# Second experts of a two-layer graph network: up to 12 units of up to 512 columns with arms chosen by token counts, rows turned by VectorE, and scatters that are not chained within an expert's unit

## The chip, the cores and the metric

The kernel runs on one core of a Trainium2 chip. A core has five engines with instruction streams of their own: TensorE (PE, with its weight loads as PEld), VectorE (DVE), ScalarE (ACT), GpSimd (POOL) and SyncE (SP). SP and ACT also issue plain DMAs, POOL also indirect ones (gathers and scatters by a list of row numbers). The metric is the device time of one execution in microseconds (us). The kernel before takes 3464.89 us, the median of three runs (3464.35 to 3468.28).

## The reference

Two layers work on 1250 rows (tokens, nodes of a graph) of 1024 float32. Each layer adds to x a graph convolution and an attention-like mix of the normalised x, then adds a mixture of experts of the normalised sum:

```python
xn = _layernorm(x)
x = x + gcn(xn, edges) + spherical_attention(xn)
x = x + experts0(_layernorm(x))          # 8 experts, capacity 391, width 512
xn = _layernorm(x)
x = x + sage(xn, edges) + linear_attention(xn)
x = x + experts1(_layernorm(x))          # the change is about this one
```

The second experts choose the two best of eight for each token and have no capacity, so that an expert can receive any number of tokens:

```python
scores = x @ gate_w.T                    # 1250 x 8
topk_scores, topk_idx = top_k(scores, 2)
p = softmax(topk_scores)
h1, h2 = split(x @ w12[e].T)             # w12[e]: 512 x 1024, two halves of 256
y += p * ((silu(h1) * h2) @ w3[e].T)     # w3[e]: 1024 x 256, for both chosen e
```

Worked out from the reference with its inputs, the eight experts of the second mixture receive 0, 276, 515, 394, 1, 557, 17 and 740 tokens, 2500 together. The first mixture's receive 318, 358, 263, 231, 330, 366, 397 and 237, of which 391 at most are kept.

## The kernel before

One function, `network`, holds the whole computation as one program. A scheduler orders the instructions of each engine; tiles from pools with a number of buffers set when a writer may start. [...] Weights of all stages share a pool of three buffers (`wpool`, tag "w"). A second call of `network` under `tc.If(many == 1)` is for inputs that do not occur here, and is not executed.

*First experts* (L780 to L899). Routing builds a table of token numbers with small matmuls (L753), and from it `idx`, `idx_q` and `taken`, the number of tokens of each expert. Expert 0's rows are gathered whole (L802), transposed by TensorE (L808) and copied by ACT and VectorE in turn (`evac`, L116 and L118). The rows of later experts are gathered as quarters of 1 KB (L816), laid out so that VectorE's 32x32 transposing (L825) gives the columns. `weights(e)` issues three loads of 2 MB on SP (gate, up, down; L844 is the down one), for expert 0 after the gathers of its rows in the program. Each engine reads `taken` into registers, and `by_width` chooses among four code arms (248, 296, 344, 392 columns) by comparing and branching: four times an expert for gate and up (L864 to L867), and twice for down (L884 to L886).

*Second routing* (L1072 to L1305). Two top scores of each token give one-hot rows; matmuls with a triangular matrix give each token's rank at its expert (`ahead`, from pR at L1158) and the experts' counts (pN). VectorE turns ranks into cells. A cell has 128 slots, and there are 27 of them (CELLS), a number that any distribution fits: ten pairs of cells with 256 slots each and seven single ones. The table of cells comes from float32 matmuls (L1292, `at` by `what`, over two choices and ten tiles of tokens) with three columns per cell: token, weight and expert. Cells that a small expert leaves partly empty are filled with tokens of weight zero: POOL computes `fill_at` (L1274), and matmuls (L1296) add it. From the table's PSUM come `unit_e` (the expert of each cell, L1298), `gate` and `idx`.

*Second experts* (L1309 to L1353). Ten pairs and seven singles form 17 units in a fixed order, each with 256 or 128 columns. A unit reads its expert's number on SP and loads w12 (2 MB, L1312) and w3 (1 MB); POOL gathers 128 rows of 4 KB per cell (L1320); TensorE transposes them (L1326), and evac copies them to `xeT`. Gate and up are 64 records of matmuls (L1333): two halves of hidden features, two banks, eight blocks of input features, each float32 matmul recorded twice. ACT applies silu, VectorE multiplies (L1337). Down is four matmuls (eight records) of 512 columns per cell (L1344); VectorE and ACT each scale half of it by the token's weight (L1349, L1347). POOL then scatters the rows with an add into the output in DRAM (L1350). All scatters write the same tensor, so each waits for the one before it to land.

Of the kernel before, what the change touches and what calls it, by code (L numbers as in the profile page):

```python
# [10 lines left out]
F32 = mybir.dt.float32  # L11
F32R = mybir.dt.float32r
# [10 lines left out]
P = 128  # L23
# [25 lines left out]
PAIRS = 10  # L49
CELLS = 27  # L50
UNITS = [u for i in range(PAIRS) for u in ((2 * i, 2), (2 * PAIRS + i, 1)) if u[0] < CELLS]
BLOCKS = 10
LN_EPS = 1e-5
# [49 lines left out]
def network(tc: tile.TileContext, a: dict, out: bass.AP, env: SimpleNamespace, exact: bool):  # L103
# [80 lines left out]
    def residual(pool, i, t, cols, bias):  # L184
# [4 lines left out]
        return xr  # L189

# [601 lines left out]
    with s_route:  # L792
        quarters = x1n_d.rearrange("n (j f) -> (n j) f", j=4)
        with tc.tile_pool(name="moe0", bufs=1) as mp:
# [34 lines left out]
            def by_width(n, widths, work):  # L829

                if len(widths) == 1:
                    return work(widths[0])
                m = len(widths) // 2
                with tc.If(n <= widths[m - 1]) as cmp:
                    by_width(n, widths[:m], work)
                with cmp.Else():
                    by_width(n, widths[m:], work)

            def weights(e):
# [4 lines left out]
                nc.sync.dma_start(wd, a["L0_ffn_down_w"][e].rearrange("(k p) f -> p k f", p=P))  # L844
# [57 lines left out]
    idx = mp1.tile([P, CELLS], I32, name="idx1")  # L902
    gate = mp1.tile([P, CELLS], F32, name="gate1")
    unit_e = mp1.tile([1, CELLS], I32, name="unit_e")
# [8 lines left out]
    expert = pk.tile([P, 2, T], F32, name="expert1")  # L913
# [171 lines left out]
    def choose1(t0, t1):  # L1085
# [3 lines left out]
        nc.vector.tensor_copy(expert[:, :, tt], ixf.rearrange("p t k -> p k t"))  # L1089
# [52 lines left out]


    with tc.tile_pool(name="cells", bufs=1) as cp:
# [6 lines left out]
        token = cp.tile([P, T], F32, name="token1")  # L1151
        nc.gpsimd.iota(token, pattern=[[P, T]], base=0, channel_multiplier=1, allow_small_or_imprecise_dtypes=True)
        count = cp.tile([P, P], F32, name="count1")
        nc.gpsimd.iota(count, pattern=[[1, P]], base=0, channel_multiplier=0, allow_small_or_imprecise_dtypes=True)
        pR = bank("pR")
# [13 lines left out]
        other = cp.tile([P, 2, E], F32, name="other")  # L1169
        nc.vector.tensor_scalar(other, both[:, 0:2, :], -1.0, 1.0, op0=OP.mult, op1=OP.add)  # L1170
# [3 lines left out]
        steps = cp.tile([P, BLOCKS], F32, name="steps")  # L1174
        nc.vector.tensor_scalar(steps, count[:, :BLOCKS], float(P), 0.5, op0=OP.mult, op1=OP.add)
        nc.vector.tensor_tensor(blocks, pN[:, :E].unsqueeze(2).to_broadcast([P, E, BLOCKS]),
                                steps.unsqueeze(1).to_broadcast([P, E, BLOCKS]), op=OP.is_gt)
        per = cp.tile([P, 3, E], F32, name="per")
        nb = cp.tile([P, E], F32, name="nb")
        nc.vector.tensor_reduce(nb, blocks, AX.X, OP.add)  # L1180
        evens = cp.tile([P, 5], F32, name="evens")
# [5 lines left out]
        for r in run:  # L1187
            nc.vector.memset(r, 0.0)
# [20 lines left out]
        def tmp(name):  # L1209
            return cp.tile([P, 2, T], F32, name=name)  # L1210
# [192 lines left out]
```

## Time and profile before

| | us |
|---|---|
| median of three runs | 3464.89 (3464.35 to 3468.28) |
| the profiled execution, own time | 3477.62 |
| its span in the trace | 3475.9 |
| TensorE busy | 3303.3 |
| VectorE, ACT, POOL busy | 915.1, 375.0, 591.1 |
| last matmul of the second graph layer ends | 3090.7 |
| first gate-and-up matmul of the second experts | 3144.17 |
| last matmul of the second experts ends | 3458.63 |
| last scatter issued | 3463.69 |

The granted TensorE clock is 0.97 of full speed in the mean. The profile is one execution, in microseconds from the start of its span. A group's row names the line, the engine, the operation, the tile written and the tiles read, shapes and count; after the bar come the busy time, the mean of one in ns, and the idle time of the engine just before the group with what ended it. Matmuls overlap in their records, so the length of a run of them is read from the timeline, where the start of one run and that of the next are seen. A line of the timeline has start, length, engine, line, operation and tiles, and in brackets the idle time before it.

### The profile page before, as it was taken

What the parts mean: (1) busy time and instruction counts of PE and PEld (TensorE: products, weight loads), DVE (VectorE), ACT (ScalarE), POOL (GpSimd) and SP (SyncE); (2) the same over time, 40 slices, a digit from 0 to 9 for tenths busy, and PEclk for the clock granted to TensorE, in tenths of its full rate; (3) what the DMA queues carried; (4) which work ended last, traced back from release to release, by engine and by line L of the source; (5) the groups of instructions that cost most, each with busy time, mean ns of one, the idle gap of its engine ahead of it and who ended that gap; (6) DMA issues with size and microseconds to landing.
All of it is one profiled execution on the core that took longest, in us unless ns stands there. A gap on an engine that the chain in (4) does not pass through costs nothing.

```text
span 3475.9 us, 31257 instructions
## 1 busy us (share of the span) xinstructions
PE 3303.3 (95%) x12399; PEld 2053.6 (59%) x12399; DVE 915.1 (26%) x2401; ACT 375.0 (11%) x662; POOL 591.1 (17%) x496
## 2 busy tenths in 40 slices
PE   6999999999998699999699999999999999988997
PEld 3474656654557456756355555457777454666775
DVE  4248335531114623231520000011111111341111
ACT  1001011100004111111110111000000000001111
POOL 0006786042001131210200000110000010022221
PEclk9999999999999599999899999999999999988999
DMA  4715222054104245554630000220100110319884
GB/s 153 170 56 130 25 1 26 25 190 139 53 25 166 76 141 196 156 184 116 212 107 25 25 25 25 93 104 1 49 1 25 64 45 18 109 57 304 277 262 102
DMA packets 165063, 343.51 MB, mean 99 GB/s; under 512 B 37467, under 2 KB 58882, under 8 KB 162684
## 3 DMA queue, kind: packets, MB, share of 16 engines
q1 hardware_dynamic: 101612, 247.26, 20.9%
q0 software_dynamic: 39616, 52.68, 7.4%
q10 hardware_dynamic: 23632, 40.77, 4.1%
q8 instruction: 138, 2.26, 0.3%
q14 instruction: 65, 0.53, 0.0%
HBM read 261.79 MB, written 78.87 MB: 98 GB/s over the span
## 4 chain that ended last, share of the span: by engine, by line
PE 52%; DMA 2%; DVE 1%; ACT 1%; issue 0%; POOL 0%; ACTq 0%; SPq 0%; POOLq 0%; DVEq 0%
PE ppn L164 8%; PE pqT L940 8%; PE p L1333 6%; PE pa L503 5%; PE ph L164 4%; PE pwo L164 4%; PE ph L1064 4%; PE py L1344 3%; PE pv L164 2%; PE py L884 2%; PE pgate L864 2%; PE pup L864 2%; DMA res_d<-xt 1%; DVE xt L971 1%; PE psc L1082 1%; PE pkv L999 1%
## 5 line engine op out<-in xcount | busy, mean ns | idle before, releaser
L265 POOL DMA_INDIRECT adj_d<-cnt,cell x167 | 259.9, 1556 | 90.7 <-issue 41.5
L1333 PE MATMUL p<-xeT,w 128*128 128x256 f32 (+1 forms) x1088 | 195.1, 340 | 5.4 <-ACT xeT L116 4.8
L1333 PEld LDWEIGHTS p<-xeT,w 128*128 128x128 f32 x1088 | 173.1, 192 | 26.3 <-ACT xeT L116 9.6
L188 POOL TENSOR_TENSOR xr<-xr,bo 128x512 f32<-128x512 f32 (+1 forms) x40 | 50.4, 1265 | 711.4 <-PE pwo L164 451.3
L864 PE MATMUL pgate<-xeT,wg 128*128 128x392 f32 (+3 forms) x512 | 154.3, 456 | 2.6 <-DVE py L886 2.0
L884 PE MATMUL py<-hT,wdb 128*128 128x392 f32 (+3 forms) x512 | 147.8, 448 | 8.2 <-DVE hT L867 4.1
L164 PE MATMUL pqk<-wk,x0T 128*128 128x512 f32 (+1 forms) x320 | 144.9, 607 | 9.5 <-ACT x0T L116 7.9
L864 PE MATMUL pup<-xeT,wu 128*128 128x392 f32 (+3 forms) x512 | 148.6, 442 | 2.2 <-issue 2.2
L164 PE MATMUL pv<-wv,x1T 128*128 128x512 f32 (+1 forms) x320 | 141.1, 598 | 7.5 <-ACT x1T L116 5.4
L164 PE MATMUL ph<-ws,h1T 128*128 128x512 f32 (+1 forms) x320 | 143.2, 596 | 0.0
L164 PE MATMUL pqk<-wq,x0T 128*128 128x512 f32 (+1 forms) x320 | 140.7, 593 | 0.0
L164 PE MATMUL ppn<-wn,x1T 128*128 128x256 f32 (+1 forms) x640 | 138.8, 379 | 0.0
L1064 PE MATMUL ph<-x1T,ws 128*128 128x416 f32 (+1 forms) x384 | 138.2, 512 | 0.0
L164 PE MATMUL pv<-wv,x0T 128*128 128x512 f32 (+1 forms) x320 | 138.0, 592 | 0.0
L164 PE MATMUL ph<-wgcn,x0T 128*128 128x512 f32 (+1 forms) x320 | 138.0, 593 | 0.0
L164 PE MATMUL pwo<-wo,attn0T 128*128 128x512 f32 (+1 forms) x320 | 137.7, 592 | 0.1
L164 PE MATMUL ppn<-wn,h1T 128*128 128x512 f32 (+1 forms) x320 | 137.7, 592 | 0.0
L164 PE MATMUL pwo<-wo,attn1T 128*128 128x512 f32 (+1 forms) x320 | 137.5, 592 | 0.0
L940 PE MATMUL pqT<-x1T,wk 128*128 128x416 f32 (+1 forms) x384 | 135.6, 512 | 0.0
L940 PE MATMUL pqT<-x1T,wq 128*128 128x416 f32 (+1 forms) x384 | 135.6, 512 | 0.0
L864 PEld LDWEIGHTS pgate<-xeT,wg 128*128 128x128 f32 x512 | 100.5, 197 | 52.6 <-issue 8.1
L884 PEld LDWEIGHTS py<-hT,wdb 128*128 128x128 f32 x512 | 97.6, 192 | 57.1 <-ACT wdb L874 6.6
(384 smaller groups left out, 4494.0 us busy)
## 6 DMA issues: line engine op xcount, KB each, us to landing
w<-in_L_ffn_w_dram SPq DMA_DIRECT2D x17, 2048.0 KB
w<-in_L_ffn_w_dram SPq DMA_DIRECT2D x17, 1024.0 KB
wg<-in_L_ffn_gate_w_dram SPq DMA_DIRECT2D x8, 2048.0 KB
wu<-in_L_ffn_up_w_dram SPq DMA_DIRECT2D x8, 2048.0 KB
wd<-in_L_ffn_down_w_dram SPq DMA_DIRECT2D x8, 2048.0 KB
y_d<-ye ACTq DMA_DIRECT2D x30, 416.0 KB
adj_d<-ezero SPq DMA_DIRECT2D x2, 6105.0 KB
res_d<-xr SPq DMA_DIRECT2D x45, 256.0 KB
```

Of the source, the lines that this page charges most:

```text
L164: nc.tensor.matmul(pr[:TS[t], :cols], xT[:, k, TOK[t]], w[:, k, :], start=(k == 0), stop=(k == nk - 1))
L188: nc.gpsimd.tensor_add(xr[:TS[t]], xr[:TS[t]], bias[:TS[t]])
L265: nc.gpsimd.indirect_dma_start(out=adj_d[e % 2], out_offset=bass.IndirectOffsetOnAxis(ap=cell[:, e:e + 1], axis=0), in_=cnt[:, e:e + 1], i ...
L503: nc.tensor.matmul(pa, edges if by_node else feats, feats if by_node else edges, start=(s == 0 and i == 0), stop=(s == T - 1 and i == len( ...
L864: nc.tensor.matmul(pw[:, :n], w[:, k, ic], xeT[:, k, :n], start=(k == 0), stop=(k == KB - 1))
L884: nc.tensor.matmul(py[:, :n], wdb[:, i, b, :], hT[:, i, :n], start=(i == 0), stop=(i == I0 // P - 1))
L940: nc.tensor.matmul(pq[:, :n], w[:, k, pair * P:(pair + 1) * P], xT[:, k, c0:c0 + n], start=(k == 0), stop=(k == KB - 1))
L971: nc.vector.scalar_tensor_tensor(xt[:ts], yt[:ts], env.wts[:ts, t, k:k + 1], xt[:ts], op0=OP.mult, op1=OP.add)
L999: nc.tensor.matmul(pkv[:, :P], kf[:TS[t], t, :], v[:TS[t], t, pair * P:(pair + 1) * P], start=(t == 0), stop=(t == T - 1))
L1064: nc.tensor.matmul(ps[:, :n], w[:, k, q0 + f * P:q0 + (f + 1) * P], xT[:, k, c0:c0 + n], start=(k == 0), stop=(k == KB - 1))
L1333: nc.tensor.matmul(pw_[:, :n], w12[:, k, off + i * P:off + (i + 1) * P], xeT[:, k, :n], start=(k == 0), stop=(k == KB - 1))
L1344: nc.tensor.matmul(py, hT[:, i, c * P:(c + 1) * P], w3[:, i, half * 512:(half + 1) * 512], start=(i == 0), stop=(i == H1 // P - 1))
```

## The change

The fixed grid of 27 cells gives way to at most 12 units (NU) of four blocks of 128 slots (UC). An expert with up to 512 tokens has one unit, one with more is shared evenly by blocks among two or three. Unit u's expert (`unit_e`) comes from the counts alone, ahead of the table. The table's matmuls are in float32r, with the weight cut into a high and a low part, in five steps behind VectorE's pieces; the filling of cells is gone. `taken` has the number of tokens of each unit, and `idx_q` the numbers of quarter rows as in the first experts.

In the units, `by_width` (moved to the top of `network`) chooses one of seven widths for gate and up in each half, and one of four numbers of blocks for gathering, turning and down. Only the first unit's rows are gathered whole and transposed by TensorE. For the others POOL gathers quarters up to two units ahead, and VectorE turns them. Units from the sixth on are skipped if empty. The first unit's weights are loaded by SP, the next two units' by ACT, the others' by SP; w12 is laid out with 16 KB in one piece for a partition. Empty slots of a table have a row number beyond the output, which the scatter leaves out, and scatters of one unit do not wait for each other.

In the first experts, the down weights of expert 0 are loaded by ACT's queue, and the load is kept in its place in the program's order. In ACT's stream as built it stands behind the four `evac` copies of expert 0's rows; POOL's stream as built has, before the units, the 12 quarter gathers of the second unit, the first block of the first unit, 8 quarter gathers of the third unit, and the other blocks of the first unit.

```diff
-PAIRS = 10
-CELLS = 27
-UNITS = [u for i in range(PAIRS) for u in ((2 * i, 2), (2 * PAIRS + i, 1)) if u[0] < CELLS]
 BLOCKS = 10
+UC = 4
+NU = 12
+COLS = NU * UC
+WIDTHS1 = [128, 192, 256, 320, 384, 448, 512]
+COUNTS = [P * (c + 1) for c in range(UC)]
...
+    def by_width(n, widths, work):
+        if len(widths) == 1:
+            return work(widths[0])
+        m = len(widths) // 2
+        with tc.If(n <= widths[m - 1]) as cmp:
+            by_width(n, widths[:m], work)
+        with cmp.Else():
+            by_width(n, widths[m:], work)
...
-                nc.sync.dma_start(wd, a["L0_ffn_down_w"][e].rearrange("(k p) f -> p k f", p=P))
+                load = (nc.sync if e else nc.scalar).dma_start(wd, a["L0_ffn_down_w"][e].rearrange("(k p) f -> p k f", p=P))
+                if e == 0:
+                    tc.keep_in_program_order(load)
...
-        fill = cp.tile([P, 2, E], F32, name="fill")
...
-        fill_at = cp.tile([P, 2, E, P], F32, name="fill_at")
-        for t in range(2):
-            for e in range(E):
-                nc.gpsimd.tensor_scalar(fill_at[:, t, e, :], count1, fill[:, t, e:e + 1], token1[:, t:t + 1],
-                                        op0=OP.is_equal, op1=OP.mult)
...
+        more = cp.tile([P, E], F32, name="more")
+        nc.vector.tensor_scalar(more, nb, UC + 0.5, None, op0=OP.is_gt)
+        units = run[0][:, 8:16]
+        nc.vector.scalar_tensor_tensor(units, nb, 0.5, more, op0=OP.is_gt, op1=OP.add)
+        nc.vector.scalar_tensor_tensor(units, nb, 2 * UC + 0.5, units, op0=OP.is_gt, op1=OP.add)
         for i, d in enumerate((1, 2, 4)):
+            nc.vector.tensor_add(run[1 - i % 2][:, 8:16], run[i % 2][:, 8:16], run[i % 2][:, 8 - d:16 - d])
+        of_unit = cp.tile([1, NU, E], F32, name="of_unit")
+        nc.vector.tensor_tensor(of_unit, count[0:1, :NU].unsqueeze(2).to_broadcast([1, NU, E]),
+                                run[1][0:1, 8:16].unsqueeze(1).to_broadcast([1, NU, E]), op=OP.is_ge)
+        its = cp.tile([1, NU], F32, name="its")
+        nc.vector.tensor_reduce(its, of_unit, AX.X, OP.add)
+        nc.vector.tensor_scalar(unit_e, its, E - 1.0, None, op0=OP.min)
...
-            for k in range(2):
-                nc.tensor.matmul(pt[:, :3 * CELLS], at[:TS[t], k, t, :], what[:TS[t], k, t].rearrange("p a g -> p (a g)"),
-                                 start=(t == 0 and k == 0), stop=False)
-        for t in range(2):
-            for e in range(E):
-                nc.tensor.matmul(pt[:, :CELLS], fill_at[:, t, e, :], fill_hit[:, e, :], start=False,
-                                 stop=(t == 1 and e == E - 1))
...
+        for t0 in range(0, T, 2):
+            tt = slice(t0, t0 + 2)
+            nc.vector.tensor_tensor(at[:, :, tt], count.unsqueeze(1).unsqueeze(1).to_broadcast([P, 2, 2, P]),
+                                    pos[:, :, tt].unsqueeze(3).to_broadcast([P, 2, 2, P]), op=OP.is_equal)
+            nc.vector.tensor_tensor(hit[:, :, tt], count[:, :COLS].unsqueeze(1).unsqueeze(1).to_broadcast([P, 2, 2, COLS]),
+                                    cell[:, :, tt].unsqueeze(3).to_broadcast([P, 2, 2, COLS]), op=OP.is_equal)
+            for j, v in enumerate((token1[:, tt].unsqueeze(1).unsqueeze(3).to_broadcast([P, 2, 2, COLS]),
+                                   w_hi[:, :, tt].bitcast(F32).unsqueeze(3).to_broadcast([P, 2, 2, COLS]),
+                                   w_lo[:, :, tt].unsqueeze(3).to_broadcast([P, 2, 2, COLS]))):
+                nc.vector.tensor_mul(what[:, :, tt, j, :], hit[:, :, tt], v)
+            for t in range(t0, t0 + 2):
+                for k in range(2):
+                    nc.tensor.matmul(pt[:, :3 * COLS], at[:TS[t], k, t, :],
+                                     what[:TS[t], k, t].rearrange("p a g -> p (a g)"),
+                                     start=(t == 0 and k == 0), stop=(t == T - 1 and k == 1))
...
+        used = cp.tile([P, COLS], F32R, name="used")
+        nc.vector.tensor_scalar(used, pt[:, :COLS], 0.5, None, op0=OP.is_gt)
+        pf = bank("pused")
+        nc.tensor.matmul(pf[:, :COLS], env.ones_r, used, start=True, stop=True)
+        took = cp.tile([1, NU], F32, name="took1")
+        nc.vector.tensor_reduce(took, pf[0:1, :COLS].rearrange("p (u c) -> p u c", c=UC), AX.X, OP.add)
+        nc.vector.tensor_copy(taken, took)
...
-        for c0, nc_ in UNITS:
-            n = nc_ * P
-            which = nc.values_load(unit_e[0:1, c0:c0 + 1], engines=(mybir.EngineType.SP,), min_val=0, max_val=E - 1)
-            w12 = wpool.tile([P, KB, 2 * H1], F32, name="w12", tag="w")
-            nc.sync.dma_start(w12, a["L1_ffn_w12"][bass.ds(which, 1)].rearrange("e (k p) f -> p (e k) f", p=P))
-            w3 = ep.tile([P, H1 // P, D], F32, name="w3")
-            nc.sync.dma_start(w3, a["L1_ffn_w3"][bass.ds(which, 1)].rearrange("e (k p) f -> p (e k) f", p=P))
-            xeT = ep.tile([P, KB, 2 * P], F32, name="xeT1")
-            for c in range(nc_):
-                xe = ep.tile([P, D], F32, name="xe1", bufs=4)
-                nc.gpsimd.indirect_dma_start(
-                    out=xe, out_offset=None, in_=env.x3n_d,
-                    in_offset=bass.IndirectOffsetOnAxis(ap=idx[:, c0 + c:c0 + c + 1], axis=0))
...
+        def load_unit(w, which, queue):
+            queue.dma_start(w[0], a["L1_ffn_w12"][bass.ds(which, 1)].rearrange("e (p k) f -> p (e k) f", k=KB))
+            queue.dma_start(w[1], a["L1_ffn_w3"][bass.ds(which, 1)].rearrange("e (k p) f -> p (e k) f", p=P))
...
+        ws = places()
+        load_unit(ws, expert_of(0, SP), nc.sync)
+        xe = ep.tile([P, UC, D], F32, name="xe1", bufs=1)
+        for c in range(UC):
+            nc.gpsimd.indirect_dma_start(
+                out=xe[:, c], out_offset=None, in_=env.x3n_d,
+                in_offset=bass.IndirectOffsetOnAxis(ap=idx[:, c:c + 1], axis=0))
+        number = [nc.values_load(taken[0:1, u:u + 1], min_val=0, max_val=UC * P) for u in range(NU)]
+        queues = [(nc.sync, SP) if u > 2 else (nc.scalar, ACT) for u in range(NU)]
+        which = [None] + [expert_of(u, queues[u][1]) for u in range(1, NU)]
+        def when(u, work):
+            if u < 5:
+                return work()
+            with tc.If(number[u] >= 1):
+                work()
+        xeT = ep.tile([P, KB, UC * P], F32, name="xeT1")
...
+        def fetch(u):
+            xq = ep.tile([P, UC * 4, B, KB], F32, name="xq1")
+            def work(n):
+                for i in range(n // B):
+                    nc.gpsimd.indirect_dma_start(
+                        out=xq[:, i].rearrange("p c b -> p (c b)"), out_offset=None, in_=quarters3,
+                        in_offset=bass.IndirectOffsetOnAxis(
+                            ap=idx_q[:, i % 4, u * UC + i // 4:u * UC + i // 4 + 1], axis=0))
+            when(u, lambda: by_width(number[u], COUNTS, work))
+            return xq
+        by_width(number[0], COUNTS, turn_first)
+        coming = [fetch(1)]
+        for u in range(NU):
+            later = u + 1 < NU
+            if u + 2 < NU:
+                coming.append(fetch(u + 2))
+            if later:
+                xq = coming.pop(0)
+                xeT2 = ep.tile([P, KB, UC * P], F32, name="xeT1")
+                ws2 = places()
+            w12, w3 = ws
+            hT = ep.tile([P, H1 // P, UC * P], F32, name="h3T")
+            def turn(n):
+                for c in range(n // P):
+                    i0, i1 = 4 * c, 4 * c + 4
+                    nc.vector.transpose(xeT2.rearrange("p b (i r) -> p i b r", r=B)[:, i0:i1],
+                                        xq[:, i0:i1].rearrange("p i c b -> p i b c"))
+            def unit():
+                if later:
+                    when(u + 1, lambda: load_unit(ws2, which[u + 1], queues[u + 1][0]))
+                for i in range(H1 // P):
+                    def gate_up(n):
+                        m = -(-n // P) * P
+                        p1, p2 = bank("p1"), bank("p2")
+                        for pw_, off in ((p1, 0), (p2, H1)):
+                            for k in range(KB):
+                                nc.tensor.matmul(pw_[:, :n], w12[:, k, off + i * P:off + (i + 1) * P], xeT[:, k, :n],
+                                                 start=(k == 0), stop=(k == KB - 1))
+                        sg = ep.tile([P, UC * P], F32, name="sg1")
+                        nc.scalar.activation(sg[:, :n], p1[:, :n], AF.Silu)
+                        nc.vector.tensor_mul(hT[:, i, :n], sg[:, :n], p2[:, :n])
+                        if n < m:
+                            nc.vector.memset(hT[:, i, n:m], 0.0)
+                    by_width(number[u], WIDTHS1, gate_up)
+                if later:
+                    when(u + 1, lambda: by_width(number[u + 1], COUNTS, turn))
+                def down(n):
+                    sent = []
+                    for c in range(n // P):
+                        ye = ep.tile([P, D], F32, name="ye1", bufs=6)
+                        own = gate[:, u * UC + c:u * UC + c + 1]
+                        for half in range(2):
+                            py = bank("py1")
+                            for i in range(H1 // P):
+                                nc.tensor.matmul(py, hT[:, i, c * P:(c + 1) * P], w3[:, i, half * 512:(half + 1) * 512],
+                                                 start=(i == 0), stop=(i == H1 // P - 1))
+                            if half:
+                                nc.scalar.activation(ye[:, 512:], py, AF.Copy, scale=own)
+                            else:
+                                nc.vector.tensor_scalar(ye[:, :512], py, own, None, op0=OP.mult)
+                        add = nc.gpsimd.indirect_dma_start(
+                            out=out, out_offset=bass.IndirectOffsetOnAxis(
+                                ap=idx_s[:, u * UC + c:u * UC + c + 1], axis=0),
+                            in_=ye, in_offset=None, bounds_check=N - 1, oob_is_err=False, compute_op=OP.add)
+                        for other in sent:
+                            tc.declare_no_dep(add.ins, other.ins, reason="no token is twice at an expert")
+                        sent.append(add)
+                by_width(number[u], COUNTS, down)
```

## The prediction

> **What bounds the kernel now.** I read the busy shares first, then the costliest groups, the chain that ended last, the stretches around the second experts, and last the order of instructions at their start and in the first experts.
>
> The page's first part and its row of TensorE's clock in 40 slices:
>
> ```profile
> PE 3303.3 (95%) x12399; PEld 2053.6 (59%) x12399; DVE 915.1 (26%) x2401; ACT 375.0 (11%) x662; POOL 591.1 (17%) x496
> PEclk9999999999999599999899999999999999988999
> ```
>
> TensorE is busy 95% of the span at nearly full clock, so in most places only fewer TensorE microseconds or a shorter gap count. Over the second experts (units from 3144 us to the end) the stretches say so too. Columns: busy time and count of PE, PEld, DVE, ACT, POOL, then clock, DMA share, GB/s.
>
> ```profile
> 3090.70:3144.20 53.50, 27.52 (x158) 25.96 (x156) 22.30 (x111) 5.17 (x10) 21.00 (x26) 0.54 0.28 102
> 3144.20:3435.70 291.50, 286.94 (x1410) 218.50 (x1411) 46.38 (x81) 39.51 (x80) 59.57 (x46) 0.99 0.83 259
> ```
>
> Routing (first row) keeps TensorE half idle. The units keep it 98% busy, with VectorE at 16%, POOL at 20%: there is room on these two to take TensorE's work. The units' groups by shape:
>
> ```profile
> L1333 PE MATMUL p<-xeT,w 128*128 128x256 f32 x640 | 143.2, 385 | 2.8 <-ACT xeT L116 2.1 <-DMA w<-in_L_ffn_w_dram 0.6
> L1344 PE MATMUL py<-w,h3T 128*128 128x512 f32 x216 | 95.5, 592 | 0.0
> L1333 PE MATMUL p<-xeT,w 128*128 128x128 f32 x448 | 51.9, 277 | 2.7 <-ACT xeT L116 2.7
> L1326 PE MATMUL pte<-ident,xe 128*128 128x128 f32 x200 | 24.4, 273 | 0.0
> ```
>
> A mean of one counts overlap, so I price by the timeline, where neighbours stand end to end (start, length):
>
> ```profile
> 3144.17 16.49 PE L1333 MATMUL p<-xeT,w 128*128 128x256 f32 x64 [0.61 <-DMA w<-in_L_ffn_w_dram]
> ...
> 3168.78 7.41 PE L1333 MATMUL p<-xeT,w 128*128 128x128 f32 x64 [0.38 <-ACT xeT L116]
> ```
>
> and by the end of the chain:
>
> ```profile
> 3437.68 14.08 PE p L1333 x64
> 3451.76 3.45 PE py L1344 x8
> ...
> 3456.19 6.72 DMA out_dram<-ye,idx
> ...
> 3463.78 1.47 POOL out_dram L1350
> ```
>
> So gate and up take 7.41 us at 128 columns and 14.08 at 256 (the first unit took 16.49: 2.4 of cold start). That is 6.67 us per 128 columns on a floor of 0.74. One block's down matmuls (eight records of 512 columns) take 3.45. The last scatter waited for the one before it to land, though its rows were ready at 3459.35.
>
> **The change, part by part.** The reference's own routing gives the second experts 0, 276, 515, 394, 1, 557, 17 and 740 tokens. The new units are thus 276; 384 and 131; 394; 1; 384 and 173; 17; 384 and 356; then two empty. Their chosen widths are 320, 384, 192, 448, 128, 384, 192, 128, 384, 384 and their blocks of 128 are 3, 3, 2, 4, 1, 3, 2, 1, 3, 3.
>
> *TensorE's stream.* Gate and up by the line above, estimates between and beyond its two rows: 128 is 7.41 (twice), 192 10.75 (twice), 320 17.4, 384 20.75 (four times), 448 24.1. Together 14.8 + 21.5 + 17.4 + 83.0 + 24.1 = 160.8. Down is 25 × 3.45 = 86.2. The sum is 247.0, plus the cold 2.4 and the gaps below. Before, from 3144.17 to the last matmul's end at 3458.63, it is 314.4 us: 10 × 14.08 + 7 × 7.41 + 27 × 3.45 = 285.8, the rest the transposes (27 × 0.88 = 23.8), the cold start and short waits. Weights drop from 17 × 3 MB to 10 × 3 MB, which I cost at nothing: a unit of 3 MB needs 7.5 us at the 400 GB/s seen at the units' start before, and the shortest real unit (7.41 + 3.45) lasts 10.86. Where a load waits for its buffer (SP from the fourth unit on, ACT for the two before), SP has only later loads behind it, ACT a silu; three buffers deep, it is a unit early.
>
> *Turning on VectorE.* One 128x1024 turn is 2.02 us (the first experts' rows below). Three blocks are 6.1 us, with multiply and output 9.5 us of a unit of some 31: hidden, and turns for the next unit stand ahead of this unit's down. One is not: from unit 5 on the turn stands between the two halves of gate and up, and unit 7 (one block) has only half of 7.41 us to hide 6.1 for unit 8, whose rows POOL issues late as well. I take 3 us (2.6 to 4), once; if all turns were exposed they would cost 22 × 2.02 = 44.
>
> *The arms.* Every engine must branch to an arm three times a unit: two gate-and-up halves and one down. The trace of before has no branch in these units but 48 arms in the first experts (8 × 6):
>
> ```profile
> L864 PE MATMUL pgate<-xeT,wg 128*128 128x392 f32 (+3 forms) x512 | 154.3, 456 | 2.6 <-DVE py L886 2.0 <-issue 0.4 <-PE pte L808 0.2
> L864 PE MATMUL pup<-xeT,wu 128*128 128x392 f32 (+3 forms) x503 | 146.7, 444 | 2.2 <-issue 2.2
> L884 PE MATMUL py<-hT,wdb 128*128 128x392 f32 (+3 forms) x448 | 133.7, 458 | 6.7 <-DVE hT L867 4.1 <-ACT wdb L874 2.5
> ...
> 1232.14 2.02 DVE L825 STREAM_TRANSPOSE xeT<-xq 128x1024 f32<-128x1024 f32 x1
> ...
> 1260.37 0.51 DVE L867 TENSOR_TENSOR hT<-sg,pup 128x344 f32<-128x344 f32 x1 [13.81 <-remote]
> ```
>
> TensorE's idle time before these arms that no data explains is 2.2 + 0.4 "issue" and the 4.1 for a multiply that VectorE began late: 6.7 us over 48 arms, 0.14 each. Ten units have 30 arms: 4.2. [...] If each of 30 arms paid the 4.1 seen above, that would be 123 us. [...] I take 4 us[...]. Stream: 247.0 + 2.4 + 3 + 4 = 256.4, against 314.4: **−58.0**.
>
> *The start of the units.* Before, weights could be asked for only at 3130.46, once the table's matmuls had told each unit's expert, and they ended the wait; the gathers were issued from 3131.27:
>
> ```profile
> 3122.46 6.75 PE ptab L1296 x32
> 3129.23 0.19 DVE unit_e L1298
> ...
> 3130.46 13.57 DMA w<-in_L_ffn_w_dram
> ```
>
> Now the expert of a unit comes from counts, some 20 small VectorE operations of about 0.1 to 0.3 us after 3102.2: near 3108, so weights land by 3125 and leave the path. The 32 fill matmuls and POOL's 15 us of fill go; the table's 40 records become 20 of a cheaper type, behind VectorE's pieces, ending near 3116; counting, spreading and the four-fold index add about 2.6 (the first experts took 2.5 from their table to that index): indices near 3119. But POOL then issues, in its new order, 12 quarter gathers of the second unit, the first block of the first unit, 8 quarter gathers of the third unit, and only then the first unit's other blocks: the third is the 24th. A gather is issued every 1.255 us:
>
> ```profile
> 3133.89 0.94 POOL L1320 DMA_INDIRECT xe<-x3n_d,idx  x1 [0.30 <-issue]
> ```
>
> 24 × 1.255 = 30.1, so 3149.5; landing takes about 4 us (an undisturbed gather in the combine was used 4.2 us after its issue ended), then 1.9 for transposes and copies: first matmul near 3155.5 against 3144.17, **+11.3**. Low end +6 (small gathers land early and VectorE's list is shorter), high end +20 (POOL's unused gathers in shorter arms wait for older ones to land). Nothing covers this stretch. For the whole kernel POOL is no bound: 92 gathers × 1.255 and 25 scatters × 1.9 are 163 us of some 300.
>
> *The first experts' start.* The 2 MB of wd for expert 0 move behind the first four evacuations on ACT's queue. Before, they were issued at 1196.84, just ahead of the four gathers of POOL, and TensorE idled:
>
> ```profile
> 1206.91 1.94 PE L808 MATMUL pte<-ident,xq 128*128 128x128 f32 x8 [10.85 <-DMA wd<-in_L_ffn_down_w_dram]
> ```
>
> The gathers end issue at 1202.5; with 4.2 us to land and the transposes, gate starts near 1209.5 rather than 1215.34: **−5.5** (0 if the gathers were slow by themselves, to −7). ACT's queue then holds the load ahead of its first silu, which needs only issue time; wd is used tens of us later.
>
> *The tail.* Scatters of one expert no longer wait for each other: the last is issued at once when its rows are ready, not 4.3 us later behind a landing[...]: **−3.3**.
>
> Sum: −5.5 + 11.3 − 58.0 − 3.3 = **−55.5**. The profiled execution's span of 3475.9 (its own time 3477.6) becomes about 3420; it stands 12.7 above the median of 3464.9, and I take the difference over: 3409.
>
> **The rivals.**
>
> 1. *Dearer start and gaps* (0.17). Unused gathers in POOL's shorter arms make it wait, +20 instead of +11, and branches cost 10 rather than 4: 3409 + 9 + 6 = 3424. For it: POOL has never been that deep in gathers before its first unit. Against: 1.255 us held in every row seen.
>
> 2. *More is won* (0.14). Evacuations and gathers run nearer +5 at the start, the first experts win 7, the arms cost nothing: 3409 − 6 − 1.5 − 4 = 3397. For it: no weights compete with the last gathers any more. Against: the 24th place of the last block is a count of instructions, not of traffic.
>
> 3. *Slower: broken prefetch* (0.05). [...] The gain without my 4 us for arms is 59.5, so it decides from 2.0 us per arm over 30 arms; at 4.1 it is 123, thus 3409 − 4 + 123 = 3528. For it: seven widths per half put more code between arms than the four of the first experts. Against: 48 arms show 0.14 each.
>
> 4. *The first experts' part does nothing* (0.07): gathers slow by themselves, 3409 + 5.5 = 3414.5; it lies within the forecast's range.
>
> **How the numbers follow.** The forecast, near 3409 (3398 to 3421 alone), has 0.57. The bounds of the start (−5 to +9), arms[...] and first experts (−1.5 to +5.5), not all at once, reach from about 3393 to 3434, and this holds the first two rivals; left out are the slower case and odd ends, 0.2 at most. A measurement here tells about 0.2%, 7 us, from no change: faster 0.94, within it 0.01 (arms at just 2 us), slower 0.05.
>
> **What would show it.** Right: no table-fill group, an L1326-like transposing group of 24 only, 25 scatters and 92 gathers; TensorE from first to last unit matmul 252 to 262 us; that first matmul 43 us or more after the index could be ready by VectorE's list, its wait ended by a gather; PE waiting for a VectorE turn before one unit only; the first experts' first gate matmul 5 us earlier. Wrong: "issue" idle of microseconds ahead of many arms; TensorE waiting for turned rows in several units (POOL or VectorE late); or a wait for weights, which I put at nothing.

## The result, and the profile after

The changed kernel takes 3455.58 us (median of seven runs), the kernel before 3466.74 us on the same chip: a ratio of 0.9966 (95% interval 0.9955 to 0.9978). Repeated on another occasion (e6_after2 below) it was 0.9980 (0.9971 to 0.9989). So it is faster by 7 to 12 us, where 55.5 were forecast. Chips differ: the kernel before has medians from 3466.74 to 3478.86, and its first experts take 452 us in one profile and 441 in another (e5_before2), with the same instructions. Ratios are therefore always to the kernel before on the same chip, and the stages below are from two profiles of one chip, e5_before2 (span 3467.4) and e6_after2 (3456.0).

| stage | before | after | difference | forecast |
|---|---|---|---|---|
| end of the first table to the first gate matmul | 22.5 | 18.0 | −4.5 | −5.5 |
| first experts | 440.6 | 439.9 | −0.7 | 0 |
| from there to the last ranking matmul | 1433.8 | 1431.9 | −1.9 | 0 |
| ranking to the first matmul of the units | 42.0 | 58.3 | +16.2 | +11.3 |
| units, first to last matmul | 312.0 | 286.2 | −25.8 | −58.0 |
| last matmul to the end of the span | 16.6 | 23.0 | +6.4 | −3.3 |

The other 1.1 us lie ahead of the first table. From the page of the first profile after (span 3458.5): TensorE's clock in 40 slices, the instruction queue (packets, MB, share; before it had 138 packets), and the group that answers to L1333.

```profile
PEclk9999999999998599999899999999999999987998
q8 instruction: 174, 2.85, 0.3%
L1386 PE MATMUL p<-xeT,w 128*128 128x384 f32 (+4 forms) x640 | 167.6, 425 | 18.0 <-issue 16.8
```

Before, these matmuls stood idle for 5.4 us, for data. Now it is 18.0, nearly all "issue": TensorE waited for nothing that the profile shows. The stretches of the units and of what follows them, with the columns as before:

```profile
3151.99:3435.28 283.29, 257.39 (x840) 152.35 (x840) 71.13 (x75) 25.11 (x45) 102.71 (x92) 0.96 0.53 150
3435.30:3458.50 23.20, 0.00 (x0) 0.00 (x0) 0.00 (x0) 0.69 (x1) 1.57 (x1) 0.55 0.26 44
```

TensorE is busy 91% of the units' time, against 98% before. Where the rest goes is seen in TensorE's timeline at the units with one and with 17 tokens (a half of gate and up is 32 records):

```profile
3275.54 3.73 PE L1386 MATMUL p<-xeT,w 128*128 128x128 f32 x32
3283.31 5.46 PE L1386 MATMUL p<-xeT,w 128*128 128x128 f32 x32 [4.04 <-issue]
3291.42 5.06 PE L1406 MATMUL py<-w,h3T 128*128 128x512 f32 x8 [2.65 <-issue]
...
3352.61 3.73 PE L1386 MATMUL p<-xeT,w 128*128 128x128 f32 x32
3361.15 6.09 PE L1386 MATMUL p<-xeT,w 128*128 128x128 f32 x32 [4.80 <-issue]
```

In these lines each arm starts 7.8 to 8.5 us after the one before, although that one held only 3.7 to 5.5 us of work. The matmuls behind a gap are slower (5.46 and 6.09 instead of 3.73), and so is the granted clock, the third number from the end in the stretches of a first half and of the two second halves:

```profile
3275.54:3279.27 3.73, 3.73 (x33) 3.54 (x31) 0.00 (x0) 0.96 (x2) 2.54 (x2) 1.00 0.67 208
3283.31:3288.77 5.46, 5.46 (x32) 5.27 (x32) 0.00 (x0) 0.28 (x1) 0.35 (x1) 0.69 0.94 181
3361.15:3367.24 6.09, 6.09 (x32) 5.90 (x32) 2.22 (x2) 0.28 (x1) 2.00 (x2) 0.61 0.49 100
```

The start of the units, POOL's gathers and TensorE:

```profile
3111.48 1.00 POOL L1350 DMA_INDIRECT xq<-x3n_d,idx_q  x1 [27.90 <-DVE idx_q L1289]
...
3129.41 0.94 POOL L1320 DMA_INDIRECT xe<-x3n_d,idx  x1 [3.16 <-DMA xq<-x3n_d,idx_q]
...
3149.03 1.97 PE L1342 MATMUL pte<-ident,xe 128*128 128x128 f32 x8 [0.24 <-DMA xe<-x3n_d,idx]
3151.99 17.46 PE L1386 MATMUL p<-xeT,w 128*128 128x320 f32 x64 [0.98 <-DVE xeT L120]
```

### The profile page after: what moved, and what is told of

Read it like the earlier page. It is cut to its first block, busy times and chain, and to the rows that moved or that the text cites. A ratio compares the mean times of both kernels' runs of the same rounds, so it can differ in the third digit from the quotient of the medians.

```text
span 3458.5 us, 30927 instructions
## 1 busy us (share of the span) xinstructions
PE 3249.1 (94%) x11696; PEld 1969.2 (57%) x11696; DVE 941.7 (27%) x2405; ACT 358.1 (10%) x622; POOL 635.5 (18%) x543
## 4 chain that ended last, share of the span: by engine, by line
PE 52%; DMA 2%; issue 1%; DVE 1%; ACT 0%; POOL 0%; another core or an unknown queue 0%; POOLq 0%; DVEq 0%; ACTq 0%; SPq 0%
PE ppn L166 8%; PE pqT L941 8%; PE pa L515 5%; PE p L1386 5%; PE ph L166 4%; PE pwo L166 4%; PE ph L1065 4%; PE pv L166 3%; PE py L1406 2%; PE py L889 2%; PE pgate L869 2%; PE pup L869 2%; PE psc L1083 1%; DMA res_d<-xt 1%; PE pkv L1000 1%
## 5 line engine op out<-in xcount | busy, mean ns | idle before, releaser
L1386 PE MATMUL p<-xeT,w 128*128 128x384 f32 (+4 forms) x640 | 167.6, 425 | 18.0 <-issue 16.8
L1386 PEld LDWEIGHTS p<-xeT,w 128*128 128x128 f32 x640 | 113.8, 201 | 73.9 <-issue 35.5
L166 PEld LDWEIGHTS ppn<-wn,x1T 128*128 128x128 f32 (+1 forms) x640 | 120.1, 188 | 17.7
```

The lines of the kernel that those rows point to most:

```text
L166: nc.tensor.matmul(pr[:TS[t], :cols], xT[:, k, TOK[t]], w[:, k, :], start=(k == 0), stop=(k == nk - 1))
L1386: nc.tensor.matmul(pw_[:, :n], w12[:, k, off + i * P:off + (i + 1) * P], xeT[:, k, :n], start=(k == 0), stop=(k == KB - 1))
```

## The experiments

Theory F: a branch to code further on leaves an engine without instructions until they are fetched. Rival B: the compares, branches and register loads themselves cost the time. Rival T: rows, weights or POOL are late. All timed runs are compared with the kernel before on the same chip.

**e1_static.** In the second experts each `by_width` and `when` is replaced by the one arm that these counts take:

```diff
-                    by_width(number[u], WIDTHS1, gate_up)
+                    known(u, WIDTHS1, gate_up)        # work(min(w for w in widths if w >= REAL[u]))
...
-            with tc.If(number[u] >= 1):
+            if REAL[u]:
                 work()
```

> The changed kernel with every choice among arms in the second experts taken out: each unit has only the one width and the one number of blocks that these inputs need, written in a straight line, and the two empty units are left out (so it serves these token counts only). Theory F (a taken branch leaves TensorE without instructions until those of the target are fetched; some 8 us pass from the start of an arm to the earliest start of the next, which only an arm with more matmul time than that hides): the 25.7 us of issue gaps between arms and the slow clock behind them go, so that first to last matmul of the units takes 250 to 256 us instead of 283, and the 23 us after the last matmul fall to about 14. Rival T (TensorE waits for rows, weights or POOL, and the gaps are only shown as issue): it stays above 275 us. In both, the straight line lets POOL gather the first unit's rows first, so the first matmul comes some 20 to 25 us earlier. Total by F about 3395, by T about 3425.

Ratio 0.9872 (0.9856 to 0.9889). No issue gap is left, and the end falls from 23 to 15.3 us, but the units took 279.8 us. The straight line let the scheduler put unit 1's turning ahead of unit 0's multiply on VectorE, where it waited for gathers:

```profile
3186.03 12.04 PE L1409 MATMUL py<-w,h3T 128*128 128x512 f32 x22 [22.15 <-DVE h3T L1393]
```

The units without the 27.9 us of such waits are 251.9 us, inside F's 250 to 256; the wait itself was in neither theory.

**e9_static2.** The same with the turning held behind the multiply, so that this wait goes:

```diff
-                        nc.vector.tensor_mul(hT[:, i, :n], sg[:, :n], p2[:, :n])
+                        mul.append(nc.vector.tensor_mul(hT[:, i, :n], sg[:, :n], p2[:, :n]))
...
-                    known(u + 1, COUNTS, turn)
+                    with tc.issue_after(mul[-1].ins):
+                        known(u + 1, COUNTS, turn)
```

> The straight line of the second experts again (only these inputs' widths and blocks, no choice among arms, the two empty units left out), with the turning of the next unit's rows held behind the multiply of this one on VectorE, so that the 22 us wait of the first straight-line run goes. Theory F: TensorE from first to last matmul of the units 249 to 256 us, as the sum of the prediction without its gaps has it (247.0 + 2.4), against 283 to 286 with arms; ratio to before 0.980 to 0.984. Rival T (rows or weights are late anyway): 265 us or more.

Ratio 0.9804 (0.9785 to 0.9822), 68 us faster than before. The units take 255.2 us, the start 38.3, the end 15.4. What TensorE still waited for in the units:

```profile
PE p L1391 <- DVE xeT L1377: 5.6, 2, 2.8
PE p L1391 <- ACT ye L1415: 1.4, 1, 1.4
```

Behind the unit of 17 tokens it is 2.8 us, the wait for the turning of unit 8's rows that the prediction put at 3; the other 2.8 is the same behind the unit of one token. T is refuted: with the same rows, weights and gathers the stream is 31 us shorter than e6_after2's.

**e2_hollow.** All compares and branches stay, and the arms not taken are empty:

```diff
+    def hollow(u, widths, work):
+
+        real = min(w for w in widths if w >= REAL[u])
+        by_width(env.number[u], widths, lambda n: work(n) if n == real else None)
...
-                    by_width(number[u], WIDTHS1, gate_up)
+                    hollow(u, WIDTHS1, gate_up)
```

> The changed kernel with all compares and branches kept, but the arms that these inputs do not choose are empty, so that an arm's code lies next to the following one's (it serves these token counts only). POOL's order at the start is as in the changed kernel. Theory F (instructions of a distant target have to be fetched): the gaps shrink to under 8 us of 25.7 and first to last matmul takes 255 to 265 instead of 283; total about 3430. Rival B (the compare, branch and register instructions themselves cost the time, some 18 a unit): the gaps stay near 25 us, total about 3455.

Ratio 0.9962 (0.9949 to 0.9974), the units 291.2 us: no gain. F's number for the gaps nearly holds: 8.4 us of issue are left, none ahead of a second half, and 6.2 of them end just when a late multiply of VectorE does. The units fetch 10 packets of 16 KB instead of 45. But TensorE waited another 25.3 us ahead of down for a late VectorE, as here (its idle time in brackets):

```profile
3184.99 0.49 DVE L1397 TENSOR_TENSOR h3T<-sg,p 128x320 f32<-128x320 f32 x1 [17.47 <-remote]
```

The inputs of this multiply were complete at about 3174.4 (the last matmul of the half). SyncE's next load was issued at 3184.91, at the same time. What held both is open. The edit also did more than it was meant to: ScalarE now loads an activation table 30 times in the units (1.28 us each), where the changed kernel does so once, and one of TensorE's long waits ends behind such a load. The total is thus no proof for F or B.

**e3_onearm.** Both halves in one arm, with twice the code between arms:

```diff
-                for i in range(H1 // P):
-                    def gate_up(n):
+                def gate_up(n):
+                    for i in range(H1 // P):
```

> The changed kernel with both halves of gate and up in one arm: ten changes of arm fewer, the same code. Theory F: the gaps ahead of second halves (about 15 us with the slow clock behind them 20) go, and those ahead of down shrink since the arm before is twice as long: 3432 to 3440. Rival B (branch instructions themselves): a third of the gaps go, about 3446. Rival T (rows or weights late): no change, 3455.

Ratio 1.0022 (1.0014 to 1.0031): slower, which no theory had. The gaps inside gate and up went, but 28.0 us of issue are left (26.6 in e6_after2), ahead of down and of the next unit (up to 7.3 us), and the units took 298.9. Down now starts 10.3, 10.8 and 14.7 us after the start of arms that hold 7.6, 7.3 and 10.6 us. A further 10.0 us are two waits of TensorE for a late VectorE, whose cause is not shown, so that the longer time is only in part that of the arms. Ten jumps fewer took nothing from the gaps: B in its plain form falls. The length of the code that is jumped over seemed to count; e10 and e11 measure that.

**e10_jump8 and e11_jump112.** The branchless kernel e8_gridturn (below), with 34 blocks that are never entered, of 8 and of 112 matmul calls (in float32 each call is recorded twice: 64 records for the 32 calls of a unit's gate and up):

```diff
+            with tc.If(never >= E):
+                for _ in range(14):          # 1 in e10_jump8
+                    pd = bank("dead")
+                    for k in range(8):
+                        nc.tensor.matmul(pd[:, :P], w12[:, k, :P], xeT[:, k, :P], start=(k == 0), stop=(k == 7))
```

> The branchless kernel with fixed cells and turned rows, and in each of its 17 units two blocks that are never entered (a compare on a register that never holds): one between the two halves of gate and up, one ahead of down. Each holds 8 matmul instructions. Both theories have 34 compares and branches. F (what costs is fetching the instructions behind a distant target): stream within 6 us of the 291 without blocks, and hardly more instruction packets. B (the branch itself costs): as much as with 112.

> The same with 112 matmul instructions in each of the 34 blocks that are never entered, as many as the seven arms of one half hold. F: instruction packets during the units rise from about 14 to 40 or more of 16 KB, and gaps of 2 to 5 us appear in the single units (halves of 3.7 us), next to none in the pairs (halves of 7 us): stream 310 to 335 us. B: as with 8 instructions.

The units take 304.4 us with 8 calls and 386.5 with 112; without blocks they were 291.1. Ratios 0.9990 (0.9981 to 0.9999) and 1.0213 (1.0185 to 1.0242). e10 is 13.3 us over the base, or 0.39 us a block (6 us were expected), e11 a further 82.1, or 2.4 us a block, well over the range given (e11 was timed twice). The instruction queue in the units of e10_jump8, then of e11_jump112:

```profile
q8 instruction: 17, 0.28, 0.4%
```

```profile
q8 instruction: 73, 1.20, 1.2%
```

What TensorE waited for in e11_jump112's units (us in total, times, longest); e10_jump8 has no wait of this kind:

```profile
PE p L1388 <- PEq L1365: 46.3, 17, 5.8
PE py L1409 <- PEq L1365: 13.6, 16, 3.2
```

All its waits come to 57 us more than e10_jump8's. The other 25 of the 82.1 are slower matmuls, at a granted clock of 0.91 instead of 0.99. A single unit of e10_jump8, and one of e11_jump112, which looks like the changed kernel's:

```profile
3200.82 8.08 PE L1388 MATMUL p<-xeT,w 128*128 128x128 f32 x64
3208.73 3.60 PE L1409 MATMUL py<-w,h3T 128*128 128x512 f32 x8
```

```profile
3216.95 3.73 PE L1388 MATMUL p<-xeT,w 128*128 128x128 f32 x32
3225.60 5.44 PE L1388 MATMUL p<-xeT,w 128*128 128x128 f32 x32 [4.92 <-PEq L1365]
3232.29 3.67 PE L1409 MATMUL py<-w,h3T 128*128 128x512 f32 x8 [1.25 <-PEq L1365]
```

Branches, registers, rows and weights are the same in both; only the code behind the branch that is not entered differs. "PEq L1365" names TensorE's own sequencer at the line of the compare. VectorE had ended its last work for this half at 3221.08, so that TensorE, which started at 3225.60, did not wait for its results. The trace has what it waited for: a packet of 16 KB of instructions was under way from 3222.89 to 3223.88, and the half began 1.72 us after it had landed. In all 19 gaps of at least 0.8 us that end at the sequencer, TensorE starts 1.62 to 1.76 us after such a packet. In the changed kernel's ten issue gaps it is 1.4 to 2.6 us. This shows F: the time, and the packets, come with the instructions that are jumped over. It also shows that 7 us of work do not always hide a jump: halves of 256 columns (7.07 us) are followed by gaps of 2.2 to 4.1 us in six of the ten pairs, where next to none were expected.

**e4_xefirst.** POOL gathers the first unit's blocks first:

```diff
+        with tc.issue_after(last_xe.ins):
+            coming = [fetch(1)]
         by_width(number[0], COUNTS, turn_first)
-        coming = [fetch(1)]
```

> The changed kernel with POOL held to gather the first unit's four blocks before the quarter rows of the second and third unit; nothing else. If the start is set by the place of the third block among POOL's gathers (24th), the first matmul comes some 25 us earlier relative to the routing and the total falls by 20 to 26, to about 3432. If the turned rows of the second unit then come late instead, TensorE waits before the second unit and the gain is 10 or less.

The start fell as expected, from 58.3 (58.9 in the first profile) to 40.0 us: the place among POOL's gathers was its cause. The total did not: ratio 0.9953 (0.9936 to 0.9970), 5 to 9 us better than the changed kernel instead of 20 to 26. The units grew to 296.5 us: issue gaps 30.4 instead of 26.6, some of 1 us between single matmuls in the second unit, and slower matmuls behind them. Why earlier gathers bring these was not tried.

**e5_before2, e6_after2.** Both kernels unchanged, for traces from one chip.

> The kernel before again, unchanged, for a trace from the same chip as the next three. In the first experts the changed kernel's trace was 10.7 us shorter from first gate to last down matmul than that of before, though the change only moves one load ahead of them. If that is a difference between chips or executions, this trace and that of the changed kernel on this chip will agree there within 3 us; if it is the change, they will differ by about 10.

> The changed kernel again, unchanged, on the same chip as the runs beside it. The gaps between arms in the second experts (25 us of issue), the start at 58 us after the last ranking matmul and the 23 us after the last matmul belong to the program and should repeat within some 5 us each; the first experts' 10.7 us should not repeat if they were chance. Ratio to before 0.995 to 0.998.

The first experts are 440.6 and 439.9 us: the 10.7 us were not the change. The gaps repeat: 26.6 us of issue in the units (25.7 in the first profile), start and end as in the table.

**e7_wdonly.** The kernel before with the load of `wd` for expert 0 on ACT's queue alone (the first part of the change's diff).

> The kernel before with only the down weights of the first expert moved to ACT's queue behind the copies. By the prediction's step the first gate matmul follows the end of the first routing table 5.5 us sooner and the total falls by 4 to 7 us (ratio 0.998 to 0.9988). If other loads or the gathers themselves hold the start, the ratio is 1.000.

Ratio 0.9985 (0.9977 to 0.9994), 5.2 us; the first gate matmul comes 17.4 us after the table instead of 22.5. TensorE's wait ahead of the first transposes, 12.28 us for `wd` in e5_before2, is now

```profile
1207.88 1.94 PE L808 MATMUL pte<-ident,xq 128*128 128x128 f32 x8 [6.26 <-issue]
```

**e8_gridturn.** The fixed units of before, with rows turned by VectorE (and, as the turned rows need it, w12 laid out as in the changed kernel; the transposing by TensorE stays for the first unit alone):

```diff
+                with tc.issue_after(mul.ins):
+                    for c in range(UNITS[u + 1][1]):
+                        i0, i1 = 4 * c, 4 * c + 4
+                        nc.vector.transpose(xeT.rearrange("p b (i r) -> p i b r", r=B)[:, i0:i1],
+                                            xq[:, i0:i1].rearrange("p i c b -> p i b c"))
```

> The kernel before with its fixed 27 cells and 17 units and no arms at all, but with the rows of all units after the first gathered in quarters and turned by VectorE, behind the multiply of the unit before. It takes the transposes from TensorE without a branch. Theory F (the change lost its gain to fetching instructions behind branches and to a late start): the 200 transposes' 23 us and the copies' short waits leave TensorE's stream, 314 to 290 us, and nothing new is paid but some 2 us for the quarter table: ratio 0.993 to 0.994, better than the changed kernel. Rival T (turned rows come too late for TensorE, POOL's 108 gathers bound the units): 314 or more, ratio at or above 1.000.

Ratio 0.9956 (0.9941 to 0.9971), somewhat less than expected: the stream is 291.1 us, as forecast, but the start is 5.9 us later: the quarter table stands ahead of POOL's first gather (some 2 us), and the gathers land later, the second one so late that TensorE waits another 2.8 us for it. Turning on VectorE is worth its price by itself, and without arms it gains at least as much as the whole change with them (0.9956 here; 0.9966 and 0.9980).

**e12_best.** The parts of the change that need no branch, for any counts:

```diff
-                nc.tensor.matmul(pt[:, :CELLS], fill_at[:, t, e, :], fill_hit[:, e, :], start=False,
+                    nc.tensor.matmul(pt[:, :128], at[:TS[t], k, t, :],       # at, what in float32r
...
-                    out=out, out_offset=bass.IndirectOffsetOnAxis(ap=idx[:, c0 + c:c0 + c + 1], axis=0),
-                    in_=ye, in_offset=None, compute_op=OP.add)
+                    out=out, out_offset=bass.IndirectOffsetOnAxis(ap=idx_s[:, c0 + c:c0 + c + 1], axis=0),
+                    in_=ye, in_offset=None, bounds_check=N - 1, oob_is_err=False, compute_op=OP.add)
```

> A kernel for any token counts without arms: the fixed 27 cells and 17 units of before, with the parts of the change that need no branch: rows turned by VectorE, the table in float32r behind VectorE's pieces and without filling (empty slots are skipped by the scatter), scatters of one unit unchained, the first expert's down weights on ACT's queue. Against the run with turned rows alone: start some 10 us sooner (fill 6.9 and faster table 3.6), first experts 5, end 2 to 4. Ratio to before 0.988 to 0.991. If the start is set by the weights (their expert is still read from the table), only half of that comes: 0.993.

Ratio 0.9901 (0.9883 to 0.9920): 34 us faster than before by the ratio (medians 3429.72 and 3467.88 us), and faster than the changed kernel. Start 30.4 us (17.6 sooner than e8, where 10 were expected), units 291.3, end 16.4 (no gain there). Against them the units of e9_static2, 255.2 us, are 36 us shorter: that much its ten units of chosen widths would be worth if the choice cost no jump.

## Why the prediction was wrong

*First experts' start, −5.5:* right; −4.5 in the stages, −5.2 in e7_wdonly.

*TensorE's sum, 247.0:* right, and so were weights at nothing: no wait for them is left in the units. The 2.4 us of cold start did not come (the first unit took 17.46 at 320 columns). The widths 320, 384, 192, 448 and 128 took 17.5, 20.8, 10.6, 24.2 and 7.3 us where gaps don't cut them, against 17.4, 20.75, 10.75, 24.1 and 7.41, and e9_static2's units are 255.2 with 7.0 of waits.

*The arms, 4 us:* this step failed, and it is the one that decides. In the first profile the units are 36.3 us over 247.0: 25.7 of issue gaps, 1.3 of other waits, and the rest (9.3) matmuls slower behind gaps; e9_static2, without arms, has none of the gaps. It is the prediction's own first sign of being wrong, issue idle of microseconds ahead of many arms. I had divided the first experts' idle time by their 48 arms, 0.14 us each, as if an arm had a fixed price. What the lines show is not a price but a time between starts: where a half of gate and up holds 3.7 to 6.1 us, the next arm starts 7.6 to 9.7 us after it began (sooner, 3.5 and 6.7 us, after the down of a single block). An arm that holds more work hides that and shows next to nothing (in the first profile 0.81 us behind a half of 384 columns that holds 10.48, and none behind the other halves of 320 to 448). The first experts' arms do: 32 records of 392 columns are some 10.5 us. The units' halves of 128 and 192 columns hold 3.7 and 5.4, and the gap is what is missing (3.73 + 4.04, 5.36 + 4.34 in the timeline). A row that I had, the first experts' groups by shape, already had the issue idle time at the narrowest arms, 248 columns, and none at 392; I averaged over it:

```profile
L864 PE MATMUL pup<-xeT,wu 128*128 128x392 f32 x192 | 65.2, 492 | 0.0
L864 PE MATMUL pup<-xeT,wu 128*128 128x248 f32 x128 | 28.4, 372 | 2.0 <-issue 2.0
```

The other end that I had, 123 us from the 4.1 us of one late multiply at each of 30 arms, I set aside because the 48 arms of before showed 6.7 us in all. The true price lay between: some 35 us in the changed kernel (the 25.7 of gaps and the 9.3 of slower matmuls), 1.2 us an arm, and 2.4 a jump in e11. Rival 3 had microseconds at an arm right and the size wrong. That TensorE starts when instructions have landed, no row of before had shown; e11's packets do.

*Turning of unit 8's rows, 3 us:* not seen in the changed kernel, whose arms are later still; seen in e9_static2 as 2.8.

*The start, +11.3:* the cause was right, the size too small: 16.2 on the chip of e5 and e6. In the first profile the first gather came 18.3 us after the ranking (17.5 forecast). POOL then waited 3.2 and 1.0 us for older gathers to land, so that its first block went out at 3129.41 instead of 3126.6, the gathers after it took 1.37 instead of 1.255 us each, and from the third block's transposes to the first matmul it was 3.0 us instead of 1.9.

*The tail, −3.3:* wrong in sign. The last scatter is indeed issued early (3436.33, 1 us after the last matmul), but the span ended 20.6 us after its issue was over. For the two empty units I had put in a microsecond, an estimate that no row showed. Without them and without arms (e9_static2) the end is 15.4 instead of 23.0: 7.6 us. Behind its last scatter the changed kernel still fetched 4 packets of instructions of 16 KB and 9 of 8 KB; that these packets are the 7.6 us is not shown. Of the 3.3 us that the early scatter was to win, 1.3 are there (15.4 against 16.6 before); the rest is open.

Put together on the chip of e5 and e6: 1.0 lost at the first start, 4.9 at the start of the units, 32.2 in the stream, 9.7 at the end, against 2.6 won in the first experts and behind them and 1.1 ahead of the table: 44.1 of the 55.5.

## What to carry to other kernels

Price a branch not by how often it is taken but by how much work of its engine lies between it and the next jump, and by how much code it jumps over: here 10 us of matmuls hid the next arm or all but 0.8 us of it, 7 us did in some places (2.2 to 4.1 us were left in six of e11's ten pairs), and 3.7 did not (4.04 and 4.80 us were left in the changed kernel); a block of 112 calls jumped over cost 2.4 us more than one of 8. One cannot read it off a place where the arms are long (0.0 us of idle time at the first experts' up matmuls of 392 columns). Arms for many sizes multiply the code that is jumped over, so a fixed grid that wastes some columns can win (0.9901 in e12 against 0.9966), and cutting the number of branches by making arms longer need not gain (1.0022 in e3). When only the choice among arms is in doubt, a straight-line version for the counts at hand tells in one run what the arms cost.

## What was not expected of the hardware

A jump past 112 matmul calls costs TensorE 2.4 us in the mean over a jump past 8 (e11 against e10), with 73 instruction packets in the units instead of 17; behind a gap TensorE starts some 1.7 us after such a packet has landed. A block of 8 that is never entered still costs 0.39 us: 64 records of 128 columns take 8.08 us in e10 and 7.31 without blocks, and why is not shown. Behind a gap a half of 128 columns took up to 6.3 us instead of 3.7, at a granted clock of 0.59 (e11). And first experts of identical code took 453 us in all four profiles of one chip and 440 in those of two others; no run here tells why.
